# A graph attention layer on one core: softplus beside the layer norm, edge values on VectorE, scatters one slot earlier, the residual two steps later, q2/k2 evictions behind the score maxima

## The chip, the core and the metric

The kernel runs on one core of a Trainium2 chip. The core has five engines that each work through a queue of their own in program order: TensorE (PE, with its weight loads listed as PEld), VectorE (DVE), ScalarE (ACT), GpSimd (POOL) and SyncE (SP, which here only starts transfers). They meet at semaphores. The metric is the device time of one execution in microseconds. Before the change the median of 3 runs is 320.62 us (320.31 to 321.89).

## What is computed

The input x is 384 nodes by 1024 features. All of it is float32.

```python
h = max(layernorm(x), 0)
q, k, v = h @ wq.T + bq, h @ wk.T + bk, h @ wv.T + bv
q2, k2, v2 = (q @ wiq.T + biq), (k @ wik.T + bik), (v @ wiv.T + biv)     # 16 heads of 64
mask = full((384, 384), -inf)
mask[src, dst] = softplus(edge_weights)[edge_type - 1]                   # 6528 edges
mask[i, i]     = softplus(edge_weights)[3] where it is still -inf
scores = q2 @ k2.T / 8 + mask
out = x + (softmax(scores) @ v2) @ wo.T + bo
```

An edge may occur more than once; the kernel makes one occurrence count by looking for repeated keys, and sends the others to a dump cell.

## The kernel before

**Precision and matmuls.** Every weight block of 128 x 1024 (a "chunk") and every activation is split into a high and a low part (`split_hi` on ScalarE, line 77; `split_lo`, line 82, on VectorE or GpSimd), and each product is three matmuls (`mm3`, lines 358 to 360). There are 56 chunks in the order v, q (8 each), iv (8), k (8), eight pairs of iq and ik, o (8). A chunk is a "slot" w: 0 to 7 are v, 8 to 15 q, 16 to 23 iv, 24 to 31 k. Slot w begins with `slot_head(w)`: the high split of w+2, the eviction of slot w-1 (`evac_row`: VectorE writes f, line 373; ScalarE the high part, line 374; VectorE the low part, line 375, after the next low split), the low split of w+2, and the load of w+4. PSUM has three banks with the name g; in the iv phase one of them holds one of the six accumulators, so that in the k phase two are in turn.

**The mask** is made beside the projections. `mask_detect` (line 211, one VectorE instruction for each of the 51 columns of 128 edges) looks for repeated keys. After each nine, `mask_index` (lines 217 and 218) writes the target cells. Then one indirect transfer for each column, started by GpSimd (`mask_scatter`, line 222), puts the 128 values into one of three tables in HBM. Columns take turns over the tables, so that scatter i waits for the landing of scatter i-3. `detect(s)` lays this out by slot: softplus in slots 0 to 2, its values on GpSimd (lines 165 to 168), the diagonal (`mask_base`, lines 204 and 206) in slot 3, detections from slot 2, three scatters in each slot from slot 4. In iv step 5, behind the 51st scatter, `mask_load` (line 232) reads the tables back into `mbs`; `mask_select` (line 236) copies them into `ma` on VectorE at the end of slots 24 (two) and 25 (one).

**The residual.** x + bo is made in HBM in six pieces: `residual(k)` in iv step k starts a load, an addition on VectorE (line 496) and a store of three successive pieces, in two buffers.

**Attention.** 48 steps, three for each of 16 heads. Step i: scores S(i) on TensorE (line 665, two banks), then VectorE adds the mask and takes the maxima (`do_ttr(i-1)`, line 671), ScalarE exp (line 675), VectorE and GpSimd the norm (`do_norm(i-3)`, lines 679 and 680), TensorE transposes (`do_T(i-5)`, line 685, two banks), ScalarE and VectorE evict them (`do_pt(i-6)`, lines 694 and 695), TensorE multiplies with v2 once a head (`do_A`, line 702). Between them `fill(r)` puts in other matmuls, in units of three with the pace RATE for each step: the iq and ik chunks (`fill_qk`), then the output projection (`fill_o`), whose pieces are released at set steps (`wready`, XSTEP + 3 = 44). At the start of an iq or ik chunk `fill_qk` also puts out the splits of w+2 and the eviction of the chunk before (`qk_done`, lines 368 and 369, and four transfers), at that place in all queues. `wo_prep` splits the o chunks in steps 37, 38, 41, 44, 47 and 51.

All of it is written with a manual schedule: each engine's queue has the order of the program text.

Of the kernel before, what the change touches and what calls it, by code (L numbers as in the profile page):

```python
# [22 lines left out]
def gnn_kernel(ctx: ExitStack, tc: tile.TileContext, x, edges, erows, etw, wq, wk, wv, wiq, wik, wiv, wo,  # L23
# [13 lines left out]
    ctx.enter_context(tc.manual_schedule())  # L37

    EB = 8
    DS, GI = 2, 3  # L40
    NTAB, RNG = 3, EC // 3
    WARM = 20

# [46 lines left out]
    xall = G3.bitcast(F32).rearrange("p a k n -> p (a k n)")  # L90
    xt = [xall[:, t * D:(t + 1) * D] for t in range(NT)]
    xn = [xall[:, (NT + t) * D:(NT + t + 1) * D] for t in range(NT)]
    for t in range(NT):
        nc.sync.dma_start(xt[t], x[t * 128:(t + 1) * 128, :])
    load(0)
    ert = work.tile([128, N], F32, tag="e", name="er", bufs=EB)
    er = ert[:EC, :256].bitcast(I32).rearrange("p (a j) -> p a j", a=2)
    nc.scalar.dma_start(er, erows)
    ed = const.tile([128, 3 * EC], I32, name="ed")
    nc.sync.dma_start(ed, edges)  # L100
    load(1)
# [33 lines left out]
        nc.gpsimd.memset(zero, 0.0)  # L135

    def mask_fill():
        nc.gpsimd.memset(ma, -3.0e38)
        for j in range(NT):
            nc.gpsimd.tensor_scalar(ma[:, j, j * 128:(j + 1) * 128], ident, 3.0e38, -3.0e38, op0=OP.mult, op1=OP.add)  # L140

    def table_clear(g):

        nc.sync.dma_start(tabs[g][:CELLS, :].rearrange("(j p m) o -> p j (m o)", p=128, m=N),
                          zero[:, None, :].to_broadcast([128, NT, N]))

    def mask_keys():
        nc.gpsimd.tensor_copy(ed.bitcast(F32), ed)
        nc.gpsimd.tensor_scalar(tmpe[:, 0, :], tmpe[:, 0, :], float(N), None, op0=OP.mult)
        nc.gpsimd.tensor_tensor(key, tmpe[:, 0, :], tmpe[:, 1, :], OP.add)  # L150

    def softplus_a():
        nc.vector.tensor_scalar(w8[:, 0:4], ew, 0.0, None, op0=OP.max)
        nc.vector.scalar_tensor_tensor(w8[:, 4:8], ew, -1.0, ew, op0=OP.mult, op1=OP.min)
        nc.scalar.activation(w8[:, 4:8], w8[:, 4:8], AF.Exp)

    def softplus_b():
        nc.scalar.activation(w8[:, 4:8], w8[:, 4:8], AF.Ln, bias=1.0)

    def softplus_c():  # L160
        nc.scalar.activation(sq, epsc, AF.Exp)
        nc.vector.tensor_tensor(w8[:, 4:8], w8[:, 4:8], w8[:, 0:4], OP.add)
        nc.vector.tensor_scalar(w8[:, 4:8], w8[:, 4:8], 8.0, 1.0e-37, op0=OP.mult, op1=OP.max)
        t, ty = tmpe[:, 0, :], tmpe[:, 2, :]
        nc.gpsimd.tensor_scalar(val, ty, 0.0, w8[:, 7:8], op0=OP.is_equal, op1=OP.mult)
        for i in range(4):
            nc.gpsimd.tensor_scalar(t, ty, float(i + 1), w8[:, 4 + i:5 + i], op0=OP.is_equal, op1=OP.mult)
            nc.gpsimd.tensor_tensor(val, val, t, OP.add)

    krt = work.tile([128, N], F32, tag="e", name="kr", bufs=EB)  # L170
    kf = ert[:EC, :256].rearrange("p (a j) -> p a j", a=2)

    def key_rows_a():
        nc.gpsimd.tensor_copy(kf, er)
        nc.gpsimd.tensor_scalar(kf[:, 0, :], kf[:, 0, :], float(N), None, op0=OP.mult)

    def key_rows_b():
        nc.gpsimd.tensor_tensor(krt[:EC, :128], kf[:, 0, :], kf[:, 1, :], OP.add)
        nc.sync.dma_start(krow, krt[:EC, :128])

    rows = {}
    PA = 6
# [51 lines left out]
    def mask_select(g):  # L234

        nc.vector.copy_predicated(ma, mbt[g].bitcast(I32), mbt[g])
# [64 lines left out]
    def warm(n):  # L301
        for i in range(n):
            ps = bank("g")
            nc.tensor.transpose(ps[:, :128], ident, ident)

    warm(WARM)
    key_rows_a()
    key_rows_b()
    load(2)
    for s in range(NTAB):  # L310
        key_load(0, s)
# [44 lines left out]

    def mm3(ps, lhi, llo, rhi, rlo, first, last):
# [62 lines left out]

    def detect(s):

        if s == 0:
            softplus_a()
        if s == 1:
            softplus_b()
        if s == 2:
            softplus_c()
        if s == 3:
            mask_base()  # L430
        if s < NTAB:
# [11 lines left out]
        if s == DS + 12:  # L443
            biv_load()

    nde = [0]
# [68 lines left out]

    def v2_evac(i):
# [23 lines left out]
    def qk_done(w):  # L540
# [12 lines left out]
        else:  # L553
# [4 lines left out]
                    nc.sync.dma_start(kf[r * 64:(r + 1) * 64, o, :, :], nf[o * 64:(o + 1) * 64, :, :])  # L558
            stacks["k", p] = ks

    def fill_qk():
        nonlocal w
        lo_sel = 0
# [24 lines left out]

# [27 lines left out]

    OT = [(0, 0), (0, 1), (1, 0), (1, 1), (2, 0), (2, 1)]
    OREADY, XSTEP = 17, 41
    now = [0]
    wready = [0, 0] + [99] * 6  # L620

    def ysum(a, c=(0, 512)):
# [115 lines left out]
    for i in range(S + LA + 4):  # L738
# [87 lines left out]
```

## Time and profile before

| | before |
|---|---|
| median of 3 runs | 320.62 us |
| the profiled execution, its own time | 321.02 us |
| its span | 319.3 us |
| PE busy | 296.7 us (93%) |
| PEld, DVE, ACT, POOL busy | 279.9, 202.4, 153.8, 167.2 us |
| the 51 scatters on POOL (line 222) | 56.8 us, mean 1114 ns |
| TensorE clock granted | full, but for one of the 40 slices |

The span runs from the first to the last instruction of the profiled execution, and the execution's own time is 1.7 us more. A busy share of PE is an average: what counts is where PE's queue has holes, and which wait ends each of them last. In the lines of a timeline the columns are start and duration in microseconds, engine, line, operation, output<-input with shapes, the number of instructions, and in brackets the idle time before and what ended it.

### The profile page before, as it was taken

What the parts mean: (1) busy time and instruction counts of PE and PEld (TensorE: products, weight loads), DVE (VectorE), ACT (ScalarE), POOL (GpSimd) and SP (SyncE); (2) the same over time, 40 slices, a digit from 0 to 9 for tenths busy, and PEclk for the clock granted to TensorE, in tenths of its full rate; (3) what the DMA queues carried; (4) which work ended last, traced back from release to release, by engine and by line L of the source; (5) the groups of instructions that cost most, each with busy time, mean ns of one, the idle gap of its engine ahead of it and who ended that gap; (6) DMA issues with size and microseconds to landing.
All of it is one profiled execution on the core that took longest, in us unless ns stands there. A gap on an engine that the chain in (4) does not pass through costs nothing.

```text
span 319.3 us, 4955 instructions
## 1 busy us (share of the span) xinstructions
PE 296.7 (93%) x1643; PEld 279.9 (88%) x1643; DVE 202.4 (63%) x487; ACT 153.8 (48%) x286; POOL 167.2 (52%) x170
## 2 busy tenths in 40 slices
PE   5999999999999993499999898999989999999995
PEld 4899999999888892499999888999889999888884
DVE  2886999987633230899932447675666685896413
ACT  2647254333322120255453466777677776876300
POOL 3692876767664756033333334563736578657010
PEclk9999999999999999599999999999999999999999
DMA  7899566445964683533348946464646475940005
GB/s 256 255 273 372 195 216 219 148 127 190 293 194 141 185 308 88 194 133 135 104 141 224 267 143 166 116 164 117 167 118 162 117 182 166 274 156 0 2 0 197
DMA packets 22197, 55.12 MB, mean 173 GB/s; under 512 B 4534, under 2 KB 8220, under 8 KB 22172
## 3 DMA queue, kind: packets, MB, share of 16 engines
q1 hardware_dynamic: 20054, 52.96, 53.9%
q0 software_dynamic: 2064, 1.80, 2.0%
q8 instruction: 13, 0.21, 0.3%
q14 instruction: 12, 0.10, 0.1%
q10 hardware_dynamic: 54, 0.05, 0.1%
HBM read 40.39 MB, written 4.97 MB: 142 GB/s over the span
## 4 chain that ended last, share of the span: by engine, by line
PE 66%; DMA 16%; POOL 5%; issue 5%; DVE 4%; ACT 2%; SPq 0%; POOLq 0%; DVEq 0%
PE g L358 16%; PE g L360 16%; PE g L359 16%; DMA tab<-val,idx 12%; PE a L702 5%; PE s L665 5%; PE t L685 5%; POOL tab L222 4%; DMA mbs<-tab 2%; DMA g<-in_x_dram 1%; DVE whl L82 1%; PE g L404 1%; DMA qs<-nat 1%; ACT nat L368 1%; DVE lnt L246 1%
## 5 line engine op out<-in xcount | busy, mean ns | idle before, releaser
L358 PE MATMUL g<-g,whl 128*128 128x384 f32 x312 | 107.6, 345 | 9.9 <-DVE f L373 9.9
L360 PE MATMUL g<-g,whl 128*128 128x384 f32 x312 | 105.3, 337 | 0.0
L359 PE MATMUL g<-g,whl 128*128 128x384 f32 x312 | 105.0, 337 | 0.0
L222 POOL DMA_INDIRECT tab<-val,idx x51 | 56.8, 1114 | 28.3 <-DMA tab<-val,idx 13.5
L358 PEld LDWEIGHTS g<-g,whl 128*128 128x128 f32 x312 | 59.3, 190 | 10.2 <-issue 10.2
L77 ACT ACTIVATE whl<-raw 128x1024 fp32r<-128x1024 f32 x51 | 53.4, 1050 | 26.2 <-DMA raw<-in_wk_dram 13.7
L680 POOL TENSOR_TENSOR e<-e,s 128x384 f32<-128x384 f32 x48 | 39.3, 828 | 49.8 <-DVE s L679 43.9
L359 PEld LDWEIGHTS g<-g,whl 128*128 128x128 f32 x312 | 59.4, 190 | 0.0
L360 PEld LDWEIGHTS g<-g,whl 128*128 128x128 f32 x312 | 59.1, 190 | 0.0
L82 DVE TENSOR_TENSOR whl<-raw,whl 128x1024 fp32r<-128x1024 f32 x41 | 50.0, 1219 | 9.1 <-ACT whl L77 9.1
L374 ACT ACTIVATE g<-f,bc 128x384 fp32r<-128x384 f32 x24 | 14.8, 617 | 63.0 <-DVE f L373 63.0
L675 ACT ACTIVATE e<-e,s 128x384 f32<-128x384 f32 x48 | 29.4, 612 | 13.5 <-DVE s L671 13.3
L82 POOL TENSOR_TENSOR whl<-raw,whl 128x1024 fp32r<-128x1024 f32 x11 | 27.1, 2463 | 15.1 <-ACT whl L77 13.6
L695 DVE TENSOR_TENSOR pt<-t,pt 128x384 fp32r<-128x384 f32 x48 | 26.3, 548 | 7.6 <-ACT pt L694 6.7
L369 DVE SCALAR_TENSOR_TENSOR nat<-g,bc,nat 128x384 fp32r<-128x384 f32 x16 | 9.9, 617 | 33.3 <-ACT nat L368 33.3
L665 PE MATMUL s<-ks,qs 128*128 128x384 f32 x96 | 25.2, 344 | 5.0 <-DVE s L671 5.0
L694 ACT ACTIVATE pt<-t 128x384 fp32r<-128x384 f32 x48 | 23.1, 481 | 9.7 <-PE t L685 9.4
L671 DVE CUSTOM_DVE_ANT_0 e<-s,ma 128x384 f32<-128x384 f32 x48 | 26.2, 548 | 1.1 <-PE s L665 0.9
L665 PEld LDWEIGHTS s<-ks,qs 128*128 128x128 f32 x96 | 17.2, 188 | 7.4 <-DVE s L671 6.6
L685 PE MATMUL t<-ident,e 128*128 128x128 f32 x144 | 23.5, 271 | 0.0
L375 DVE SCALAR_TENSOR_TENSOR g<-f,bc,g 128x384 fp32r<-128x384 f32 x24 | 21.1, 884 | 0.7 <-ACT g L374 0.7
L524 POOL TENSOR_TENSOR vhl<-tv,vhl 128x512 fp32r<-128x512 f32 x6 | 9.2, 1537 | 23.3 <-ACT vhl L523 23.3
(147 smaller groups left out, 435.7 us busy)
## 6 DMA issues: line engine op xcount, KB each, us to landing
ks<-nat SPq DMA_DIRECT2D x32, 192.0 KB, 3.5
raw<-in_wv_dram SPq DMA_DIRECT2D x8, 512.0 KB, 6.3
raw<-in_wq_dram SPq DMA_DIRECT2D x8, 512.0 KB, 3.5
raw<-in_wiv_dram SPq DMA_DIRECT2D x8, 512.0 KB, 4.1
raw<-in_wk_dram SPq DMA_DIRECT2D x8, 512.0 KB, 5.2
raw<-in_wiq_dram SPq DMA_DIRECT2D x8, 512.0 KB, 3.4
raw<-in_wik_dram SPq DMA_DIRECT2D x8, 512.0 KB, 4.0
raw<-in_wo_dram SPq DMA_DIRECT2D x8, 512.0 KB, 4.7
```

What stands on the lines that cost most here:

```text
L77: nc.scalar.activation(dst[0], raw[w], AF.Copy)
L82: (eng or nc.vector).tensor_tensor(lo, raw[w], hi.bitcast(F32), OP.subtract)
L222: nc.gpsimd.indirect_dma_start(out=tabs[c // RNG], out_offset=bass.IndirectOffsetOnAxis(ap=idx[:, c:c + 1], axis=0), in_=val[:, c:c + 1], ...
L358: nc.tensor.matmul(ps, lhi, rhi, start=first, stop=False)
L359: nc.tensor.matmul(ps, lhi, rlo, start=False, stop=False)
L360: nc.tensor.matmul(ps, llo, rhi, start=False, stop=last)
L665: nc.tensor.matmul(ps[:, :N], qs[:, o, t * 128:(t + 1) * 128], ks[:, o, s, :], start=(s == 0), stop=(s == 1))
L671: nc.vector.tensor_tensor_reduce(e, st_ps.pop(i)[:, :N], ma[:, t, :], -0.125, 3.0e38, OP.add, OP.min, s[:, 0:1])
L675: nc.scalar.activation(es[i], es[i], AF.Exp, bias=s[:, 0:1], scale=-1.0, accum_out=s[:, 1:2])
L680: nc.gpsimd.tensor_tensor(es[i], es[i], s[:, 2:3].to_broadcast([128, N]), OP.mult)
L685: nc.tensor.transpose(ps[:, k * 128:(k + 1) * 128], es[i][:, k * 128:(k + 1) * 128], ident)
L695: nc.vector.tensor_tensor(lo, pv, hi.bitcast(F32), OP.subtract)
```

## The change

The parts, in the order of the program:

- The edge rows are loaded as 128 x 102 instead of 51 x 256 values, by SP behind the first tile of x instead of by ScalarE; `key_rows` works on that form and writes the same keys to HBM. `mask_consts` moves to the start of GpSimd's queue.
- Softplus: `softplus_a` goes between the low parts of the layer norm on VectorE; Exp, Ln and the Exp that restores the table follow each other on ScalarE behind the high split of chunk 1; `softplus_c` follows on VectorE.
- The values of the edges (nine instructions on 128 x 51) go from GpSimd to VectorE, in slot 1. The low splits of chunks 3 and 4 go from VectorE to GpSimd.
- Detections are 3 in slot 1, 6 in slot 2, then 4; scatters start in slot 3; `mask_load` stands in iv step 4.
- `mask_fill` and `mask_base` go from GpSimd's queue ahead of the scatters to right behind `mask_load`.
- `residual(k)` runs in slot 18 + k, the last two in k slots 0 and 1.
- In the attention the head of an iq or ik chunk becomes a task, run in each step behind `do_norm`. RATE goes from 7.6 to 7.9.

```diff
+    ert = work.tile([128, N], F32, tag="e", name="er", bufs=EB)
+    er = ert[:, :2 * EC].bitcast(I32)
     for t in range(NT):
         nc.sync.dma_start(xt[t], x[t * 128:(t + 1) * 128, :])
+        if t == 0:
+            nc.sync.dma_start(er, erows)
     load(0)
-    ert = work.tile([128, N], F32, tag="e", name="er", bufs=EB)
-    er = ert[:EC, :256].bitcast(I32).rearrange("p (a j) -> p a j", a=2)
-    nc.scalar.dma_start(er, erows)
...
+    def mask_floats():
+        nc.gpsimd.tensor_copy(ed.bitcast(F32), ed)
+
     def mask_keys():
-        nc.gpsimd.tensor_copy(ed.bitcast(F32), ed)
...
-        nc.scalar.activation(w8[:, 4:8], w8[:, 4:8], AF.Exp)
-
     def softplus_b():
+        nc.scalar.activation(w8[:, 4:8], w8[:, 4:8], AF.Exp)
         nc.scalar.activation(w8[:, 4:8], w8[:, 4:8], AF.Ln, bias=1.0)
+        nc.scalar.activation(sq, epsc, AF.Exp)
...
+    def mask_values():
         t, ty = tmpe[:, 0, :], tmpe[:, 2, :]
-        nc.gpsimd.tensor_scalar(val, ty, 0.0, w8[:, 7:8], op0=OP.is_equal, op1=OP.mult)
+        nc.vector.tensor_scalar(val, ty, 0.0, w8[:, 7:8], op0=OP.is_equal, op1=OP.mult)
         for i in range(4):
-            nc.gpsimd.tensor_scalar(t, ty, float(i + 1), w8[:, 4 + i:5 + i], op0=OP.is_equal, op1=OP.mult)
-            nc.gpsimd.tensor_tensor(val, val, t, OP.add)
+            nc.vector.tensor_scalar(t, ty, float(i + 1), w8[:, 4 + i:5 + i], op0=OP.is_equal, op1=OP.mult)
+            nc.vector.tensor_tensor(val, val, t, OP.add)
...
+    mask_consts()
     warm(WARM)
-    key_rows_a()
-    key_rows_b()
+    key_rows()
...
     ln_lo(2, 0, p2[0])
+    softplus_a()
     ln_lo(0, 1, p0[1])
     ln_lo(1, 1, p1[1])
     ln_lo(2, 1, p2[1])
     ln_rstd()
+    mask_floats()
     split(1, nc.gpsimd)
-    mask_consts()
+    softplus_b()
+    softplus_c()
     mask_keys()
-    mask_fill()
...
-        split_lo(w + 2)
+        split_lo(w + 2, nc.gpsimd if w in (1, 2) else None)
...
     def detect(s):
-        if s == 0:
-            softplus_a()
         if s == 1:
-            softplus_b()
-        if s == 2:
-            softplus_c()
-        if s == 3:
-            mask_base()
+            mask_values()
...
-        if s == DS:
-            detects(5)
-        elif s > DS:
-            detects(4)
-        if s >= DS + 2:
+        detects((0, 3, 6)[s] if s < 3 else 4)
+        if s >= 3:
             scatters(3)
...
         scatters(3)
-        residual(k)
-        if k == 5:
+        if k == 4:
             mask_load()
+            mask_fill()
+            mask_base()
+        if k >= 2:
+            residual(k - 2)
...
         for g in {0: (0, 1), 1: (2,)}.get(m, ()):
             mask_select(g)
+        if m < 2:
+            residual(m + 6)
...
+    tasks = []
+    def run_tasks():
+        while tasks:
+            tasks.pop(0)()
+    def qk_head(w):
+        load(w + 4)
+        split_hi(w + 2)
+        if pendq:
+            pendq.pop(0)()
+        split_lo(w + 2, nc.gpsimd if (w + 2) % 2 == PAR else None)
     def fill_qk():
         nonlocal w
         for p in range(8):
             for n in ("iq", "ik"):
-                load(w + 4)
-                split_hi(w + 2)
-                if pendq:
-                    pendq.pop(0)()
-                split_lo(w + 2, nc.gpsimd if (w + 2) % 2 == PAR else None)
+                tasks.append(lambda w=w: qk_head(w))
+                if now[0] < 0:
+                    run_tasks()
...
-        pendq.pop(0)()
+        tasks.append(lambda: pendq.pop(0)())
...
-    PRE, RATE, RATE_O, RATE_E = 84, 7.6, 8, 8
+    PRE, RATE, RATE_O, RATE_E = 84, 7.9, 8, 8
...
             do_norm(i - 3)
+        run_tasks()
         if 0 <= i - LT < S:
             do_T(i - LT)
```

More of the change, by code (lines that the diff above doesn't have):

```diff
@@ L39, in gnn_kernel @@
     EB = 8
-    DS, GI = 2, 3
+    GI = 3
     NTAB, RNG = 3, EC // 3
@@ L154, in softplus_a, with softplus_b, key_rows @@
         nc.vector.scalar_tensor_tensor(w8[:, 4:8], ew, -1.0, ew, op0=OP.mult, op1=OP.min)
+    def softplus_b():
         nc.scalar.activation(w8[:, 4:8], w8[:, 4:8], AF.Exp)
-    def softplus_b():
         nc.scalar.activation(w8[:, 4:8], w8[:, 4:8], AF.Ln, bias=1.0)
+        nc.scalar.activation(sq, epsc, AF.Exp)
     def softplus_c():
-        nc.scalar.activation(sq, epsc, AF.Exp)
         nc.vector.tensor_tensor(w8[:, 4:8], w8[:, 4:8], w8[:, 0:4], OP.add)
         nc.vector.tensor_scalar(w8[:, 4:8], w8[:, 4:8], 8.0, 1.0e-37, op0=OP.mult, op1=OP.max)
+    def mask_values():
         t, ty = tmpe[:, 0, :], tmpe[:, 2, :]
-        nc.gpsimd.tensor_scalar(val, ty, 0.0, w8[:, 7:8], op0=OP.is_equal, op1=OP.mult)
+        nc.vector.tensor_scalar(val, ty, 0.0, w8[:, 7:8], op0=OP.is_equal, op1=OP.mult)
         for i in range(4):
-            nc.gpsimd.tensor_scalar(t, ty, float(i + 1), w8[:, 4 + i:5 + i], op0=OP.is_equal, op1=OP.mult)
-            nc.gpsimd.tensor_tensor(val, val, t, OP.add)
+            nc.vector.tensor_scalar(t, ty, float(i + 1), w8[:, 4 + i:5 + i], op0=OP.is_equal, op1=OP.mult)
+            nc.vector.tensor_tensor(val, val, t, OP.add)
     krt = work.tile([128, N], F32, tag="e", name="kr", bufs=EB)
-    kf = ert[:EC, :256].rearrange("p (a j) -> p a j", a=2)
-    def key_rows_a():
+    kf = ert[:, :2 * EC]
+    def key_rows():
         nc.gpsimd.tensor_copy(kf, er)
[L175 to L179, printed above, removed]
+        nc.gpsimd.tensor_scalar(kf[:, :EC], kf[:, :EC], float(N), None, op0=OP.mult)
+        nc.gpsimd.tensor_tensor(krt[:, :EC], kf[:, :EC], kf[:, EC:], OP.add)
+        nc.sync.dma_start(krow.rearrange("c j -> (c j)").rearrange("(p e) -> p e", p=128), krt[:, :EC])
     rows = {}
@@ L436, in detect @@
             key_load(2, s - 7)
-        if s == DS:
-            detects(5)
-        elif s > DS:
-            detects(4)
-        if s >= DS + 2:
+        detects((0, 3, 6)[s] if s < 3 else 4)
+        if s >= 3:
             scatters(3)
-        if s == DS + 12:
+        if s == 14:
             biv_load()
@@ L559, in qk_done @@
             stacks["k", p] = ks
+    tasks = []
[8 more added lines that the diff above has]
+        split_lo(w + 2, nc.gpsimd if (w + 2) % 2 == PAR else None)
     def fill_qk():
         nonlocal w
-        lo_sel = 0
         for p in range(8):
             for n in ("iq", "ik"):
-                load(w + 4)
-                split_hi(w + 2)
-                if pendq:
-                    pendq.pop(0)()
-                split_lo(w + 2, nc.gpsimd if (w + 2) % 2 == PAR else None)
+                tasks.append(lambda w=w: qk_head(w))
+                if now[0] < 0:
+                    run_tasks()
                 gps[w] = bank("g")
@@ L618, in gnn_kernel @@
     OREADY, XSTEP = 17, 41
-    now = [0]
+    now = [-1]
     wready = [0, 0] + [99] * 6
@@ L805 @@
             [np.asarray(a).reshape(EC, 128).T for a in (src, dst, edge_type_5)], axis=1)),
-        "erows": np.ascontiguousarray(np.stack([np.asarray(a).reshape(EC, 128) for a in (src, dst)], axis=1)),
+        "erows": np.ascontiguousarray(np.concatenate([np.asarray(a).reshape(128, EC) for a in (src, dst)], axis=1)),
         "etw": np.asarray(L0_gnn_edge_type_weights),
```

## The prediction, made before the changed kernel ran

> **What bounds the kernel now.** PE is busy for 93% of the span, so I read first who PE waits for: the waits of its queue, longest in total first (total, times, longest, in us).
>
> ```profile
> PE g L358 <- DVE f L373: 9.9, 1, 9.9
> PE s L665 <- DVE s L671: 5.0, 5, 1.6
> ```
>
> Beyond the first 14 us only these two reasons make holes. The first is one hole. PE's timeline shows it:
>
> ```profile
> 122.02 0.34 PE L360 MATMUL g<-g,whl 128*128 128x384 f32 x1
> 132.23 0.66 PE L358 MATMUL g<-g,whl 128*128 128x384 f32 x1 [9.87 <-DVE f L373]
> ```
>
> The columns are start, duration, engine and line, operation, and the idle time before. The matmul at 132.23 would have started at 122.20 (pitch 0.173 us elsewhere): 10.0 us lost. The 14 matmuls after it take 4.3 us, not 2.4: another 1.9. The hole costs 11.9. VectorE's timeline says why: its queue stood before the mask.
>
> ```profile
> 128.28 1.43 DVE L236 COPY_PREDICATED ma<-mbs 128x1152 f32<-128x1152 int32 x1 [12.27 <-DMA mbs<-tab]
> 130.21 1.43 DVE L236 COPY_PREDICATED ma<-mbs 128x1152 f32<-128x1152 int32 x1 [0.51 <-DMA mbs<-tab]
> 131.54 0.54 DVE L373 TENSOR_TENSOR f<-g,rrow 128x384 f32<-128x384 f32 x1
> ```
>
> The f at 131.54 frees the bank that slot 26 needs. Before it stand the table reads, and before those the scatters. GpSimd's timeline, the scatters 1, 28, 37, 46 and 51 and the reads:
>
> ```profile
> 39.09 1.26 POOL L222 DMA_INDIRECT tab<-val,idx  x1 [0.36 <-DVE junk L211]
> ...
> 80.04 0.96 POOL L222 DMA_INDIRECT tab<-val,idx  x1 [0.31 <-issue]
> ...
> 97.28 0.96 POOL L222 DMA_INDIRECT tab<-val,idx  x1 [2.00 <-DMA tab<-val,idx]
> ...
> 111.52 0.96 POOL L222 DMA_INDIRECT tab<-val,idx  x1 [0.30 <-issue]
> ...
> 122.92 0.96 POOL L222 DMA_INDIRECT tab<-val,idx  x1 [0.30 <-issue]
> 123.88 2.37 POOL L232 DMA_DIRECT2D mbs<-tab  x3
> ```
>
> So 1.52 us for each of the first 27, 1.75 over the next 18, 2.28 over the last five. The floor is 0.96 + 0.30 of issue; the rest is mostly landings (2.1 to 6.2 us), for which the third scatter after waits. The five holes in the attention have this form on VectorE:
>
> ```profile
> 177.11 0.62 DVE L369 SCALAR_TENSOR_TENSOR nat<-g,bc,nat 128x384 fp32r<-128x384 f32 x1 [3.89 <-ACT nat L368]
> 177.64 1.22 DVE L82 TENSOR_TENSOR whl<-raw,whl 128x1024 fp32r<-128x1024 f32 x1
> 178.77 0.55 DVE L671 CUSTOM_DVE_ANT_0 e<-s,ma 128x384 f32<-128x384 f32 x1
> ```
>
> The eviction waits for a chunk's end with a split behind it, and the maxima that free the bank stand behind both. By PE's start times the five cost 5.8 us.
>
> **What the Trainium skill says.** "TensorE: Matmul & The Clock Gate", Part 1: after an idle window of about 3.4 us PE's clock is halved, for about as long. The trace agrees (0.32 for 0.173 us after 9.87 idle; nothing after holes up to 1.6). "SBUF — State Buffer", Who interferes with whom: VectorE and GpSimd share a port pair under an exclusive lock, taken by tensor_scalar, or by two SBUF inputs against a reading GpSimd instruction. The trace agrees: a tensor_scalar on 128x3 (line 259) takes 2.02 us beside a GpSimd low split. "ScalarE: Activation LUTs", What ACT_TABLE_LOAD costs: 1.28 us plus a drain; here 1.28, and 1.5 with the small activation. "DMA: Bandwidth & Descriptors", Issuing engines are not separate DMA queues: all transfers share 16 engines, which fits the landings.
>
> **The change part by part.**
>
> *Start.* The erows issue ahead of x tiles 1 and 2 delays them by some 0.45 us; VectorE took x0 and x1 without a pause, so up to 0.5 reaches PE. `mask_consts` fits into 4.1 us of GpSimd's idle time. I take +0.2 (0 to 0.5).
>
> *Softplus.* ScalarE: three table loads with their activations, 3 x 1.5 = 4.5 us, from 15.8 to 20.2; then the high split of chunk 2 to 21.2, its low split to 22.4. Slot 2 needs it at 23.1. Cost nothing, with 0.6 us of cover.
>
> *Values and first detections.* VectorE from f(0) at 22.7: f 0.55, nine value instructions some 1.5 (0.15 to 0.2 each, from lines 162 and 163), nine detections 2.65, f 0.55, two low parts 1.1, index 0.45: 29.5. To that comes the lock: GpSimd's low splits of chunks 3 and 4 (2.4 each, from 22.4 and about 25) block the tensor_scalars by 1.6 to 4 us. The index is ready at 31 to 33.5; f(1) comes by 30.2 (slot 4 needs it at 31.3), the low split of chunk 5 by 35.2 (needed at 35.5): hidden, narrowly. GpSimd is free at 27.4, so the first scatter goes out at about 32.5 instead of 39.1.
>
> *Scatters.* 27 x 1.52 bring the 28th to 73.5. The next nine now come before the residual traffic (from about 85): 9 x 1.52, 87.1. The last 14 run beside it as 18 did before: 14 x 1.75 = 24.5. The 51st starts at 111.6. At 1.52 throughout it would be 108.4; with 2.28 at the end and a late start, 115.5.
>
> *Fill and diagonal.* Off the queue's start they hid; now they follow the reads. From the 51st: 0.96 + 2.37 (reads) + 2.4 (line 138, 140) + 2.7 (lines 204, 206: three pairs of 0.9) = 8.4. The reads land sooner (5.4 and 7.2 before). Two selects 2.8, a residual addition 0.6, f 0.55: 12.4 from the 51st to the free bank, 9.2 before. So f ends at 124.0, and PE, out of work at 122.4, idles 1.7 us, too short for the clock. Gain 11.9 - 1.9 = 10.0. A 51st at 108.4 gives the whole 11.9; at 115.5 PE idles 5.5, perhaps half the clock loss: gain 5.5.
>
> *Residual.* Each piece takes some 5.7 us (its load waits for the store two pieces earlier, about 5 us to land). SP can start at 85.2 instead of 79.3, so the last addition can run at 118, before the second select ends at 122.8: hidden. The low splits behind the additions had 4 us and more of cover (6 for chunk 26). In v2_evac the second tv waits for the last store, landing at about 128: up to 1 us of VectorE, within its slack.
>
> *Evictions behind the maxima.* The maxima no longer stand behind them, so the five holes go: -5.8. What is late next are the transposes' low parts behind eviction and split: end of chunk + 0.6 + 0.62 + 1.22 + 0.55 = 3.0 us, when the next transpose can ask for the bank 2.1 us later: 0.8, expected once or so.
>
> *RATE 7.9.* PE gets 384 - 84 = 300 units in 38.0 steps, not 39.5. But the output pieces are held until step 44: steps 41 to 43 are left without filler. At the last eviction, now in step 37, it also stands before VectorE's cast of o chunk 2. From S(37): chunk end 1.0, eviction 2.3, low part 2.9, aof 3.4, cast 4.1; then GpSimd as here:
>
> ```profile
> 265.82 2.40 POOL L82 TENSOR_TENSOR whl<-raw,whl 128x1024 fp32r<-128x1024 f32 x1 [1.38 <-issue]
> 268.17 0.83 POOL L680 TENSOR_TENSOR e<-e,s 128x384 f32<-128x384 f32 x1
> 268.95 1.01 POOL L718 TENSOR_TENSOR g<-aof,g 128x384 fp32r<-128x384 f32 x1
> 269.92 2.41 POOL L82 TENSOR_TENSOR whl<-raw,whl 128x1024 fp32r<-128x1024 f32 x1
> ```
>
> and norm(36) 0.83: 11.6. PE reaches T(36) after 9.4 (10.2 before, when the norm was there after 9.0). So PE waits 2.2 us. I take +2.2 (0 to 3), and +0.5 for small waits. Attention: -5.8 + 0.8 + 2.7 = -2.3 (-5 to 0).
>
> Sum: +0.2 - 10.0 - 2.3 = -12.1. Against the profiled execution: span 319.3 to 307.2, its time 321.02 to 308.9. The median lies 0.4 lower: 320.62 - 12.1 = 308.5 us.
>
> **Rivals.**
>
> *Landings set the pace.* The scatters start earlier into the table clears and key rows, and the last 14 meet the residual's stores; at 2.28 us each they end at 119 and f at 131.4: the hole is 9 us with its clock loss, gain about 1 there and 2.3 in the attention: 317. For it: 2.28 at the end before. Against: 1.58 from 37 to 46, beside the same residual. Halfway, a 51st at 115.5: 313.
>
> *All hidden.* 51st by 109 and no wait in step 41: -11.9 - 5 + 0.2, about 304. For it: nine undisturbed scatters ran at 1.41 (67.3 to 80.0). Against: 12.4 us from scatter to bank, and no filler in three steps.
>
> *Slower: the mask's tail on GpSimd.* Fill and diagonal add 3.2 us between last scatter and bank. If the scatters end as late as before because landings alone set them, f ends at 135.3, 3.2 later; without a gain in the attention that is 324. It decides from a 51st at about 123, with 2.3 gained elsewhere from 124. Against: a start 6 us earlier must all be lost.
>
> **How the numbers follow.** Likeliest case 0.62 (own range 305.5 to 312); landings 0.22 (312 to 318); all hidden 0.10 (303 to 305.5); slower 0.06. Together 304.5 to 315 holds eight in ten, leaving out the ends of the second and third and the last. Within 0.5% (1.6 us, about what a measurement tells from no change) falls little of the landings case: 0.03; slower 0.05; faster 0.92.
>
> **What would show it.** First scatter at 31 to 34, 51st at 108 to 115.5; the hole before slot 26 under 4 us with full clock after; selects released by GpSimd's line 212 and not by the reads; no wait of PE for the maxima; a wait of about 2 us for a norm near step 41. A 51st after 119, or new holes in slots 2 to 7, would make the forecast wrong.

## The result, and the profile after

The changed kernel takes 318.98 us (median of 22 runs, 316.21 to 321.44); the kernel before, on the same chips, 320.5 us (22 runs, 318.0 to 323.79). The ratio is 0.9953, with the interval 0.993 to 0.9977: 1.5 us faster, where 12.1 had been forecast. The medians here and in the table below are over all runs; the ratios leave out the runs that took over 1.5% more than the fastest of their kernel. The profiled execution has a span of 317.1 us (319.3 before) and took 318.8 us.

PE's queue first, as before: what it waits for (total, times, longest, in us).

```profile
PE g L366 <- DVE f L381: 8.2, 1, 8.2
...
PE t L699 <- POOL e L694: 2.6, 2, 1.7
...
PE t L699 <- DVE pt L709: 0.8, 1, 0.8
```

The wait for the maxima is gone altogether. The transposes now wait for the norms (line 694) and once for an eviction. And the wait for f, which was to fall under 2 us, is still there: PE's timeline shows the same hole in the same place.

```profile
122.72 0.34 PE L368 MATMUL g<-g,whl 128*128 128x384 f32 x1
131.23 0.66 PE L366 MATMUL g<-g,whl 128*128 128x384 f32 x1 [8.17 <-DVE f L381]
```

By start times 8.3 us are lost, and 2.0 in slow matmuls behind it: 10.3. Before it was 12.1, not the 11.9 of the forecast: the 4.3 us behind that hole hold 13 matmuls, which take 2.25 at full speed, and not 14. The mask's own chain on GpSimd (the scatters 1, 28, 37 and 51, the first and third table read, the fill, the end of the diagonal):

```profile
34.06 1.24 POOL L228 DMA_INDIRECT tab<-val,idx  x1 [6.37 <-DVE idx L224]
...
76.65 0.96 POOL L228 DMA_INDIRECT tab<-val,idx  x1 [2.00 <-DVE g L383]
...
91.55 1.91 POOL L228 DMA_INDIRECT tab<-val,idx  x1 [2.17 <-DMA tab<-val,idx]
...
116.41 0.96 POOL L228 DMA_INDIRECT tab<-val,idx  x1 [0.30 <-issue]
117.37 0.83 POOL L238 DMA_DIRECT2D mbs<-tab  x1
...
121.71 0.75 POOL L238 DMA_DIRECT2D mbs<-tab  x1 [2.54 <-DMA tab<-val,idx]
122.44 1.08 POOL L140 MEMSET ma<- 128x1152 f32 x1
...
126.66 0.45 POOL L212 TENSOR_TENSOR ma<-ma,d 128x128 f32<-128x128 f32 x1
```

And what VectorE does with it:

```profile
127.14 2.90 DVE L242 COPY_PREDICATED ma<-mbs 128x1152 f32<-128x1152 int32 x2 [13.45 <-POOL ma L212]
129.94 0.68 DVE L495 TENSOR_TENSOR xh<-xh,bot 128x512 f32<-128x512 f32 x1
130.53 0.55 DVE L381 TENSOR_TENSOR f<-g,rrow 128x384 f32<-128x384 f32 x1
```

The 51st scatter starts 6.5 us earlier than before (116.41 for 122.92), but f ends only 1.0 earlier (131.08 for 132.08). From the 51st to the end of f it was 9.2 us and is 14.7; I call this stretch the tail. The new link is at 121.71: the third table read waits for the 51st scatter to land, 5.3 us behind its start, and fill and diagonal stand in GpSimd's queue behind that read. In the kernel before, the three reads went out in one piece without a wait, so the last landing took 2.6 us at most (122.92 to the third read at 125.49). The DMA engines tell the two stretches apart. From the 51st scatter to the third read, before and then after (stretch, length, busy time of PE, PEld, DVE, ACT and POOL with instructions, PE clock, DMA share, GB/s):

```profile
122.92:125.49 2.57, 0.00 (x0) 0.00 (x0) 0.00 (x0) 0.00 (x0) 2.56 (x4) 1.00 0.14 13
```

```profile
116.41:121.71 5.30, 5.30 (x33) 5.30 (x32) 0.00 (x0) 0.00 (x0) 2.56 (x4) 1.00 0.83 260
```

Three differences make up the span's: hole with its slow matmuls -1.8, attention -1.1 (five holes of 5.8 gone, 4.7 come), start +0.7 (the matmul behind the hole was due at 122.89, not 122.20). Together -2.2, and the span fell by 2.2.

### The profile page after: what moved, and what is told of

Its sections match the earlier page's. It is cut to its first block, busy times and chain, and to the rows that moved or that the text cites. A ratio compares the mean times of both kernels' runs of the same rounds, so it can differ in the third digit from the quotient of the medians.

```text
span 317.1 us, 4954 instructions
## 1 busy us (share of the span) xinstructions
PE 297.0 (94%) x1643; PEld 279.4 (88%) x1643; DVE 204.3 (64%) x494; ACT 154.8 (49%) x286; POOL 166.5 (53%) x163
## 4 chain that ended last, share of the span: by engine, by line
PE 69%; DMA 12%; issue 6%; POOL 6%; DVE 3%; ACT 3%; SPq 0%; DVEq 0%; POOLq 0%
PE g L366 17%; PE g L368 17%; PE g L367 17%; DMA tab<-val,idx 10%; PE a L716 5%; PE s L679 4%; PE t L699 4%; POOL tab L228 3%; DMA g<-in_x_dram 2%; PE g L412 2%; POOL e L694 1%; ACT nat L376 1%; DVE whl L82 1%; DVE pt L709 1%; ACT e L689 1%
## 5 line engine op out<-in xcount | busy, mean ns | idle before, releaser
L228 POOL DMA_INDIRECT tab<-val,idx x51 | 58.2, 1141 | 31.5 <-DMA tab<-val,idx 12.1
L694 POOL TENSOR_TENSOR e<-e,s 128x384 f32<-128x384 f32 x48 | 40.2, 846 | 49.0 <-DVE s L693 43.1
L82 DVE TENSOR_TENSOR whl<-raw,whl 128x1024 fp32r<-128x1024 f32 x39 | 47.6, 1221 | 13.5 <-ACT whl L77 13.5
L82 POOL TENSOR_TENSOR whl<-raw,whl 128x1024 fp32r<-128x1024 f32 x13 | 32.0, 2460 | 17.5 <-ACT whl L77 13.0
L699 PEld LDWEIGHTS t<-ident,e 128*128 128x128 f32 x144 | 18.2, 140 | 7.7 <-POOL e L694 3.2
L376 ACT ACTIVATE nat<-g,bc 128x384 fp32r<-128x384 f32 x16 | 9.3, 582 | 26.2 <-PE g L368 20.2
```

The source lines that it names most:

```text
L82: (eng or nc.vector).tensor_tensor(lo, raw[w], hi.bitcast(F32), OP.subtract)
L228: nc.gpsimd.indirect_dma_start(out=tabs[c // RNG], out_offset=bass.IndirectOffsetOnAxis(ap=idx[:, c:c + 1], axis=0), in_=val[:, c:c + 1], ...
L694: nc.gpsimd.tensor_tensor(es[i], es[i], s[:, 2:3].to_broadcast([128, N]), OP.mult)
L699: nc.tensor.transpose(ps[:, k * 128:(k + 1) * 128], es[i][:, k * 128:(k + 1) * 128], ident)
```

## The experiments

The table gives, for every kernel, the scatters and f in its profiled execution, and the sum of the waits for landings that GpSimd's timeline shows ahead of the last 14 scatters (each with the 0.3 us of issue that every scatter has). All in us; "tail" is the 51st start to the end of f.

| kernel | 1st | 28th | 37th | 51st | waits, last 14 | tail | PE hole | median | ratio to before (interval) |
|---|---|---|---|---|---|---|---|---|---|
| before | 39.1 | 81.3 | 98.6 | 122.9 | 6.2 | 9.2 | 10.0 | 320.5 | |
| changed | 34.1 | 76.7 | 91.6 | 116.4 | 5.2 | 14.7 | 8.3 | 318.98 | 0.9953 (0.993 to 0.9977) |
| e1 fill early | 34.9 | 78.5 | 94.6 | 119.1 | 5.5 | 12.1 | 8.6 | 317.48 | 0.987 (0.9791 to 0.9949) |
| e2 RATE 7.6 | 33.6 | 77.3 | 92.7 | 116.3 | 3.5 | 13.8 | 8.4 | 316.23 | 0.9873 (0.9795 to 0.9951) |
| e3 no residual | 33.8 | 76.8 | 92.0 | 112.7 | 2.4 | 13.2 | 3.2 | 311.1 | 0.9672 (0.9596 to 0.9748) |
| e4 six tables | 33.6 | 70.8 | 89.5 | 107.5 | 0.0 | | | 336.92 | 1.0496 (1.0433 to 1.0559) |
| e5 no additions | 33.0 | 76.6 | 93.0 | 119.4 | 9.0 | 11.4 | 10.0 | 319.55 | 0.9975 (0.9949 to 1.0) |
| e6 residual back | 34.3 | 76.4 | 92.0 | 119.0 | 8.8 | 11.8 | 8.5 | 319.86 | 0.9982 (0.9954 to 1.0009) |
| e7 residual late | 33.9 | 77.3 | 90.8 | 110.9 | 1.4 | 13.3 | 2.2 | 314.44 | 0.9813 (0.9737 to 0.9888) |
| e8 four together | 34.0 | 76.2 | 90.5 | 110.4 | 0.8 | 13.7 | 2.3 | 309.3 | 0.9672 (0.9622 to 0.9723) |
| e10 the same, residual a step earlier | 33.6 | 77.3 | 92.4 | 112.7 | 4.0 | 11.2 | 2.5 | 307.78 | 0.9594 (0.956 to 0.9628) |
| e11 the same, fill behind the reads | 32.8 | 75.2 | 89.1 | 109.3 | 1.5 | 13.3 | 1.7 | 306.66 | 0.9573 (0.953 to 0.9615) |
| f1 before + attention part | 38.5 | 78.7 | 96.3 | 121.1 | 7.8 | 9.4 | 8.2 | 319.98 | 0.999 (0.9964 to 1.0016) |
| f1b before + attention part, RATE 7.6 | 38.9 | 79.8 | 97.1 | 121.9 | 6.3 | 8.9 | 9.0 | 316.03 | 0.9841 (0.9786 to 0.9895) |
| f2 before + residual late | 39.0 | 79.9 | 94.2 | 114.7 | 3.7 | 10.2 | 2.9 | 316.29 | 0.9866 (0.9824 to 0.9908) |
| f3 = f1b + f2 | 39.0 | 82.5 | 97.0 | 119.1 | 5.2 | 8.9 | 6.1 | 312.45 | 0.9719 (0.9667 to 0.9771) |

The profiled executions of e1, e3, e4 and f3 took clearly longer than their medians (320.13, 314.38, 341.38 and 316.57 us), so their rows may show a later 51st than most of their executions have. All but the last two columns are of one execution.

### Is it the fill and the diagonal behind the reads? (e1)

```diff
+        if s == 2:
+            mask_fill()
+            mask_base()
...
             mask_load()
-            mask_fill()
-            mask_base()
```

> The changed kernel, with the fill and the diagonal of the mask put into GpSimd's queue before the first scatter (in its idle time from 27.7 to 34.1) and not behind the three table reads. Theory: behind the 51st scatter's landing (121.4) two things stand in a row, the third table read and then the fill and diagonal, and the selects wait for the second. With them early the selects are released by the table read, f ends about 9.3 behind the start of the 51st scatter in place of 14.7, TensorE's hole at the mask falls from 8.3 to 3-4 and its slow matmuls with it: 4 to 6.5 us faster than the changed kernel, 312.5 to 315. Rival, landings alone: the last read lands where the fill and diagonal end anyhow, and the time moves by 1 us at most, 318 to 319.

317.48 us: 1.5 us under the changed kernel's median, with intervals that overlap, and so neither of the two. The trace shows why the question stayed open. GpSimd's timeline and then VectorE's:

```profile
122.63 2.42 POOL L238 DMA_DIRECT2D mbs<-tab  x3 [2.60 <-DMA tab<-val,idx]
```

```profile
127.03 1.43 DVE L242 COPY_PREDICATED ma<-mbs 128x1152 f32<-128x1152 int32 x1 [13.32 <-DMA mbs<-tab]
```

The tail did fall from 14.7 to 12.1, and the selects are released by the reads, as expected. But even the first read waited until 122.63, and in this execution the 51st stood at 119.1, 2.7 later; the hole stayed at 8.6. The place at the front may have a cost of its own: the first scatter waits for VectorE's index in both traces, and it starts at 34.9 with the fill beside VectorE's values and at 34.1 without.

### Is it the residual? (e3, e5, e6)

e3 leaves the residual's bias out of the computation (the last stage adds x alone), e5 leaves out the additions of bo only, e6 has the residual at the steps of the kernel before.

```diff
# e3
-        if k >= 2:
-            residual(k - 2)
...
-        if m < 2:
-            residual(m + 6)
...
-            nc.sync.dma_start(xb[t], xbd[t * 128:(t + 1) * 128, :])
+            nc.sync.dma_start(xb[t], x[t * 128:(t + 1) * 128, :])
# e5
-                nc.vector.tensor_tensor(xh[i], xh[i], xh["b"][:, c], OP.add)
# e6
-        if k >= 2:
-            residual(k - 2)
+        residual(k)
...
-        if m < 2:
-            residual(m + 6)
```

> The changed kernel without the addition of the bias bo to x and without its stores (this part of the computation is left out; the last stage adds x alone). Theory: the last 14 scatters run at 1.77 us because VectorE's residual adds and their stores share SBUF and the queues with GpSimd's descriptor work; without them 1.5 each, the 51st at about 112.5 in place of 116.4, and 3.5 to 5 us off the time. Rival: the pace of the scatters is their own (landings, or GpSimd's work on the descriptors); the 51st moves by less than 1 us and the time by less than 1.

> The changed kernel without VectorE's six additions of bo in the residual (left out of the computation); its loads of x, of bo and its stores stay. Leaving out the whole residual put the 51st scatter at 112.7 in place of 116.4. Theory: the scatters' landings queue behind the residual's 256 KB loads and stores; without the adds alone the 51st stays at 115.5 to 117.5 and the time within 1.5 us of the changed kernel. Rival: the adds on VectorE hold GpSimd up (six adds of 0.68 us, one beside every second or third scatter); the 51st comes to 112 to 114 and the time falls by 4 to 9.

> The changed kernel with the residual's loads, adds and stores two steps earlier, where the kernel before has them. Theory: the traffic delays the landings wherever it meets them, so the 51st scatter stays at 115 to 117; but the last stores are gone when the last scatter lands and the table reads run, so f ends 12.5 behind the 51st in place of 14.7: hole 5.5 to 6.5, 2 to 4 us faster than the changed kernel. Rival: the place makes no difference (within 1 us).

Without the residual the 51st starts at 112.7, as the theory had it, and the time falls by 7.9 us, more than expected. Up to the 37th scatter nothing differs (92.0 for 91.6). The last 14 take 20.8 us for 24.9: of the 4.1 us saved, 2.0 are idle time of GpSimd between the scatters (5.9 for 7.9), and 2.1 are the scatters' own instructions (14.9 for 17.0). e5 tells the additions from the transfers. Without the additions the scatters' instructions are short too (14.5), but the idle time grows to 11.8, and the time stays (319.55): shorter instructions buy nothing while landings are late. The last scatter of all waited longest. GpSimd's timeline of e5:

```profile
119.35 0.96 POOL L228 DMA_INDIRECT tab<-val,idx  x1 [3.34 <-DMA raw<-in_wk_dram]
```

So it is not VectorE's additions, which the theory of e3 had named as well; it is the transfers. The wait is put down to a weight load, which is the last transfer to end, not one that a scatter depends on; 119.35 is outside the 115.5 to 117.5 that I had expected, on the side of the theory.

e6 misses the theory's 2 to 4 us: at its old place the residual costs the same (319.86, waits of 8.8 us in the last 14). Its last stores are gone earlier, and the tail is shorter (11.8), but the last 14 scatters take 27.1 us for 24.9; the two steps that the change moves the residual by are worth nothing that shows.

SyncE's timeline of the changed kernel shows what the 51st scatter (116.41) has to land among:

```profile
114.77 0.33 SPq L493 DMA_DIRECT2D xh<-in_x_dram  x1
115.15 1.63 SPq L65 DMA_DIRECT2D raw<-in_wk_dram  x1
116.87 0.38 SPq L497 DMA_DIRECT2D xbd<-xh  x1
117.34 0.38 SPq L65 DMA_DIRECT2D raw<-in_wk_dram  x1
```

That is 256 + 512 + 256 + 512 KB issued within 2.6 us. From 117 to 123 the engines moved 303 GB/s; at this rate the 1.57 MB are worth 5.2 us, by estimate, and the landing took 5.3. A third of it, 512 KB, is the residual's.

### The residual behind the mask (e7), also alone on the kernel before (f2)

```diff
-        if k >= 2:
-            residual(k - 2)
...
-        if m < 2:
-            residual(m + 6)
+        residual(m)
...
-                t = work.tile([128, 2, N], F32R, tag="nat", name="xh", bufs=2)
-                xh[i] = t.bitcast(F32).rearrange("p a n -> p (a n)")[:, :512]
+                xh[i] = xh["r"][i % 2]        # the spare 2 KB of the two bias tiles
```

> The changed kernel with the whole residual six steps later, in the eight steps of the k projection, behind the mask (its three transient tiles lie in the spare 2 KB of the two bias tiles). Theory: as without the residual, the last scatters run free of its traffic, the 51st at 112 to 113.5, hole at the mask 0 to 3.5: 308.5 to 312. Rival: VectorE's adds and the loads then delay the k projection, which gives 2 us or more back: 312 to 316, with new waits of TensorE between 135 and 165.

> The kernel before, its scatters starting at 39.1 as ever, with the residual alone moved behind the mask into the steps of the k projection. Theory: the 28th scatter stays at 81.3 and the 23 behind it take 34 us in place of 41.6, so the 51st stands at 115 to 116.5 in place of 122.9; behind it 12 to 13.5 us of landing, reads and selects, because the weight loads now go on: f at 128 to 129.5, hole at the mask 6 to 7.5 in place of 10, 3 to 5.5 us faster than before. Rival: the early start of the scatters is what is needed; without it the late residual gives less than 2 us.

All of the computation is there again, and the 51st starts at 110.9. The work by stretches of the changed kernel, and then of e7, from 92 to 110 us (stretch, length, busy time of PE, PEld, DVE, ACT and POOL with instructions, PE clock, DMA share, GB/s):

```profile
92.00:110.00 18.00, 18.00 (x81) 14.90 (x80) 8.13 (x9) 4.24 (x4) 12.78 (x11) 1.00 0.62 184
```

```profile
92.00:110.00 18.00, 18.00 (x81) 14.90 (x80) 4.90 (x4) 4.26 (x5) 12.96 (x14) 1.00 0.40 124
```

TensorE does the same; the DMA engines are busy 0.40 of the time in place of 0.62, and GpSimd gets 14 instructions off in place of 11. The hole is 2.2 us, and the matmuls behind it run at full clock. The median is 4.5 us under the changed kernel's, not the 7 to 10 expected: it lies in the rival's range. TensorE has two new waits, 0.6 us at 150 for VectorE's f and 1.7 at 166 for the first shifted copies of k2, which is the 2 us that the rival named.

f2 puts the same move alone on the kernel before, with the scatters starting at 39.0 as before. 316.29 us, 4.1 faster, within the 3 to 5.5 expected: the 51st at 114.7 is earlier than in the changed kernel, which starts 5 us sooner. Over all profiled executions the waits of the last 14 scatters are 3.5 to 9.0 us with the residual beside them and 0.8 to 4.0 without, but for f3 with 5.2. The hole (2.9) is smaller than expected, because the tail was 10.2 and not 12 to 13.5.

### The attention (e2, f1, f1b)

```diff
-    PRE, RATE, RATE_O, RATE_E = 84, 7.9, 8, 8
+    PRE, RATE, RATE_O, RATE_E = 84, 7.6, 8, 8
```

e2 is this line on the changed kernel. f1 is the kernel before with the tasks and 7.9, f1b with the tasks and 7.6.

> The changed kernel with RATE 7.6 in place of 7.9 (the spacing by which the planner of the attention steps spreads its tasks). Theory: the 3.1 us that TensorE waits for the norms of two late steps (270 and 273), and the 1.6 for eviction and maxima, come from the plan running ahead of GpSimd's norms; by the rows of the trace 1.4 to 2 us of the 4.7 stay. 2.5 to 3 us faster than the changed kernel, 316. Rival: the norms are late because GpSimd is slow, whatever the plan; the time stays within 0.5 us.

> The kernel before with the attention part of the change alone (evictions of q2/k2 as tasks behind the maxima, RATE 7.9). The prediction gave this part 2.3 us; the rows of the changed kernel give 5.8 less 4.7 = 1.1. Theory: 1 us faster than before (319.5, ratio 0.997), the five waits for the maxima gone and the two for the norms (1.7 and 0.9) there as in the changed kernel. Rival: the norms are late only behind the changed front of the kernel; without it 2 to 4 us faster.

> The same with RATE 7.6, the value of the kernel before. Theory: 5.8 less 1.6 = 4.2 us faster than before (316.4, ratio 0.987): the reordering is worth what it removes, and the step from 7.6 to 7.9 gives most of it away. Rival: RATE is worth less than 1 us here, ratio 0.994 or more.

PE's waits in f1:

```profile
PE t L695 <- POOL e L690: 2.6, 2, 1.7
...
PE t L695 <- DVE pt L705: 0.8, 1, 0.8
```

and in f1b:

```profile
PE t L695 <- DVE pt L705: 1.2, 2, 0.8
```

The same two waits for norms as in the changed kernel, behind another front; so they belong to this part. By start times the waits of the attention are 4.7 us in f1 and 1.5 in f1b. With 7.9 the part is worth nothing that can be told from no change (0.999); with 7.6 4.4 us by the medians (0.9841). e2 took 3.1 us off the attention's waits in its trace (4.7 to 1.6), and its median stands 2.7 under the changed kernel's, though with overlapping intervals. The theory holds in all three: the reordering is good, and the step of RATE that came with it pays most of it back.

### The landings' own pace (e4)

Every second group of three scatters goes to three spare tables, which nothing reads, so half of the edges are missing from the mask.

```diff
+    spare = [dram.tile([CELLS + 128, 1], F32, name=f"spare{g}") for g in range(NTAB)]
...
-        nc.gpsimd.indirect_dma_start(out=tabs[c // RNG],
+        nc.gpsimd.indirect_dma_start(out=(spare if i // NTAB % 2 else tabs)[c // RNG],
```

> The changed kernel with every second group of three scatters sent to three spare tables, which are neither cleared nor read (so half of the edges are left out of the mask); a scatter then waits only for the landing of the sixth before it, not of the third. Theory 'landings set the pace': 1.3 to 1.4 us each in place of 1.58 to 1.77, the 51st at 98 to 105, TensorE's hole at the mask is gone, and 8 to 10.5 us come off. Theory 'GpSimd's own work sets the pace': 1.5 to 1.75 each as before, the 51st at 113 to 117 and less than 3 us off.

As to the scatters the first theory is right: 1.38 us each up to the 28th (1.58 in the changed kernel) without one wait for a landing, and the 51st at 107.5, although the 37th stood 6.6 us waiting for VectorE. As to the time both are wrong: 336.92, 18 us more than the changed kernel. PE's waits:

```profile
PE g L367 <- issue: 7.3, 11, 1.8
...
PE g L369 <- issue: 6.0, 7, 1.6
PE g L368 <- issue: 4.9, 7, 0.9
```

and ScalarE's timeline:

```profile
73.29 0.61 ACT L383 ACTIVATE g<-f,bc 128x384 fp32r<-128x384 f32 x1 [13.37 <-issue]
```

18.2 us in pieces of about one, and 13.4 in one, in which TensorE and ScalarE waited for nothing that the profile shows, between 53 and 111 us, while the DMA engines were 0.17 busy from 52 to 88. By start times TensorE loses some 28 us there, for its clock is down too (0.65 from 52 to 88); the mask's 10.3 are gone, and so about 18 remain. These stops come with six scatters in flight, and with three they are not there. By what way, these runs don't show; it stays open. What e4 does show is that with three in flight landings set the scatters' pace and not GpSimd's work, and that the spare tables are no way out.

### Together (e8, e10, e11, f3)

e8 is e7 with the early fill of e1, RATE 7.6 and the edge rows' load back on ScalarE's queue; e10 has the residual one step earlier on top; e11 is e10 with fill and diagonal behind the reads again, where the change has them. f3 is f1b and f2 in one, without anything the change does ahead of the mask.

```diff
# e8, ahead of load(0)
-        if t == 0:
-            nc.sync.dma_start(er, erows)
+    nc.scalar.dma_start(er, erows)
# e10
+        if k == 7:
+            residual(0)
...
-        residual(m)
+        if m < 7:
+            residual(m + 1)
# e11
-        if s == 2:
-            mask_fill()
-            mask_base()
...
             mask_load()
+            mask_fill()
+            mask_base()
```

> Late residual, fill and diagonal before the first scatter, RATE 7.6, and the load of the edge rows back on ScalarE's queue. Theory: hole at the mask gone and TensorE's clock full (10 off), attention waits 1.4 to 2 in place of 4.7 (2.6 to 3 off), start 0.5 to 0.7 earlier: 304 to 307. If the landings of the last scatters still set the end of the mask, 307 to 311.

> As with all four together (309.3), with the residual one step earlier: its first loads in the last step of the iv projection, its last store one step before the end of the k projection. Theory: the 1.4 us that TensorE waits for the first shifted copies of k2 at 167 are due to the last residual store and its buffers; they go, 307.5 to 308.5. Rival: that wait is that of the copies themselves, 309 to 310; or the first loads meet the table reads and the hole at the mask grows by up to 1 us.

> The fastest version so far (late residual one step earlier, RATE 7.6, edge rows on ScalarE's queue), with fill and diagonal behind the table reads again, where the change has them. Theory: fill and diagonal end 5.3 behind the last read's issue, the first two reads land about 4.5 behind it when the weight loads go on; so the selects come 1 to 5 us later than with the early fill, f ends at 125 to 128 in place of 123.9, 1 to 4 us slower (309 to 312). Rival: landings alone set it, within 0.7 us.

> The kernel before with the late residual and the attention part at RATE 7.6, without everything the change does ahead of the mask (scatters from 39.1 as before). The two alone gave 4.3 and 5.1. Theory: they add, since one is the mask's hole and one the attention's waits: 310.5 to 312, so that the earlier scatters are worth 3 to 4 us of the fastest version's 307.8. Rival: the gains overlap, 313 or more.

e8 gave 309.3 us, which is the second of its two expectations, that landings still set the end of the mask: a hole of 2.3 us was left. In e10 the wait for the copies at 166 us fell from 1.4 to 0.3, as expected, and the time to 307.78. e11 answers the question of e1 for the time: with fill and diagonal behind the reads it is not slower (306.66; the intervals of e10 and e11 overlap, and the ratios are 0.7 us apart). The theory is out, the rival right as to the time. GpSimd's timeline of e11:

```profile
109.28 0.96 POOL L227 DMA_INDIRECT tab<-val,idx  x1 [1.49 <-DMA bot<-in_x_dram]
...
112.97 0.75 POOL L237 DMA_DIRECT2D mbs<-tab  x1 [1.12 <-DMA tab<-val,idx]
```

and VectorE's:

```profile
118.44 3.13 DVE L241 COPY_PREDICATED ma<-mbs 128x1152 f32<-128x1152 int32 x2 [6.20 <-POOL ma L211]
122.05 0.56 DVE L380 TENSOR_TENSOR f<-g,rrow 128x384 f32<-128x384 f32 x1
```

The selects are released by the diagonal at 118.4, 5.5 us behind the last read's issue. In e10, with the fill early, they start at 118.2, only 1.5 behind it. So the fill does lengthen the tail (13.3 for 11.2), but in e11's trace the 51st stands 3.5 us earlier, at 109.3. Of these 0.8 are there from the first scatter on (32.8 for 33.6), as between e1 and the changed kernel; where the rest comes from, one trace of each doesn't show. In e8, with the fill early too, the selects waited for the reads until 120.5, 5.3 behind the last one.

f3 has a median of 312.45, a little above the expected 310.5 to 312; by its ratio, 0.9719, it is 311.5, inside. The gains add up: by their ratios f2 and f1b save 4.3 and 5.1 us, and f3 saves 9.0. So all that the change does ahead of the mask (softplus, values, the scatters 5 us earlier) is worth 4.0 to 4.7 us by the ratios (f3 against e10 and e11, which have the edge rows on ScalarE's queue and the k2 copies earlier as well), once the residual is out of the way and RATE is put back. The interval of f3 alone is 1.7 us to either side.

e11 beats both kernels: 306.66 us, 4.3% under the kernel before.

## Why the prediction was wrong

**The step that failed is the mask's end: "The 51st starts at 111.6" and "12.4 from the 51st to the free bank".** It gave f at 124.0; f ended at 131.1, late by 4.8 at the 51st and by 2.3 behind it. The hole gave back 1.8 us where 10.0 were forecast: 8.2 of the 9.9 us that are missing between the profiled executions.

- *Start of the scatters*, 32.5 forecast: 34.06, +1.6. The lock is a part of it. The Trainium skill ("SBUF — State Buffer", Who interferes with whom) has VectorE and GpSimd share a port pair that a tensor_scalar can take for itself. The trace agrees: the two of them beside GpSimd's low splits took 1.73 and 2.39 us (0.24 otherwise), 3.6 lost, near the upper end of the 1.6 to 4 that I gave and 0.8 above its middle. The other 0.8 I have not traced.
- *"27 x 1.52"*: a miscount of mine. The rows called the 28th, 37th and 46th are the 27th, 36th and 45th of the kernel before. 40.95 us for 26 steps are 1.575 each, and the changed kernel has 1.577. +1.6. With the right count the chain says 113.7, so this slip alone doesn't explain the miss. It is in two other figures: the last stretch before has six steps, so 1.90 us each and not 2.28, and the undisturbed scatters from 67.3 to 80.0 have eight, so 1.59 and not 1.41.
- *"9 x 1.52"*: 1.66. +1.2. *"14 x 1.75"*: 1.78. +0.4. These four make the 51st 4.8 late.
- *The tail*: the terms of fill, diagonal, selects, addition and f were right within 0.4 us in sum. Missing was a wait: the third read for the 51st's landing, 2.5 us and a pause of 0.2 before. I had written that "the reads land sooner", and had asked this of the reads only, not of the landing which they wait for.

**What the sum held at nothing: "Residual ... hidden".** I priced its additions on VectorE and the arrival of its pieces. Its transfers share the DMA engines with the landings that the scatters and reads wait for. e3 and e7 show what that costs: 3.7 and 5.5 us at the 51st scatter, f at 125.9 and 124.2 in place of 131.1, and 7.9 and 4.5 us of the time. The kernel before has the same loss, and f2 gets 4.1 us back from it without any earlier scatter. A part of this was in the forecast without my seeing it: "14 x 1.75" was measured beside the residual, and it came nearly right. So the residual is no further term of the 4.8 us; it is a cost that the forecast carried along, and it bears on the tail's missing wait. That f in e7 falls on the forecast's 124.0 is luck: there the last 14 scatters took 20.1 us in place of 24.5, which makes up for a 37th that is 3.7 late and a tail that is 0.9 longer.

**The short tail before was no property of the mask.** I took 9.2 us from the kernel before and added the fill. But its 51st came at 122.9, when the transfers were nearly over: the last two weight loads went out at 113.5 and 116.0, and SP starts the next at 133.2. In the changed kernel the last of them went out at 117.3, behind the 51st, and the next at 132.2. It is not TensorE that ends the loads (it ran until 122.4 and 123.1); in both kernels VectorE has stood still before the selects, since 116.0 and 113.7. Split at the third read, the tails of the fifteen kernels with three scatters in flight fall into groups:

- From the 51st to the third read it is 2.6 to 3.0 us where the DMA engines are 0.09 to 0.26 busy (before, f1, f1b, f3, e5, e6), and 3.7 to 5.3 where they are 0.58 to 0.96 busy (all others, e1 among them). That the traffic does it is argued from these shares; no run took the weight loads away.
- From the third read to the first select it is 5.4 to 5.5 us wherever fill and diagonal stand behind the reads, and 0.8 to 3.3 where they come early, but for e8 with 5.3, where the reads themselves were late.

**Fill and diagonal.** 3.2 us on the tail by the forecast; e1 showed 2.6 and the pair of e10 and e11 2.2, between e7 and e8 it was nothing (13.3 and 13.7). In the time no pair shows a cost that is clear of the intervals. The place matters less than the working said.

**The attention** was right in kind: five holes gone (5.8 us), a late low part (0.9 and three of 0.2, forecast 0.8 and 0.5), the wait for the norm near step 41 (2.0, forecast 2.2). A second wait for the next norm, 1.1 us, was not in the sum; so -1.1 in the trace in place of -2.3.

**The start** came 0.7 later in place of 0.2. In seven executions with the changed start the last matmul ahead of the hole begins between 120.7 and 122.7, in five with the start of before between 121.8 and 122.3, so 0.5 can't be read from one trace. In the three kernels with the edge rows on ScalarE's queue it is 120.9 to 121.7.

**Softplus** was hidden, as forecast: its three table loads, 1.28 us each, left no hole.

**The rivals.** "Landings set the pace" named the right mechanism, with 0.22. It put f at 131.4, and f came at 131.1, but by luck: its 51st, at 119 from the wrong 2.28, was 2.6 too late, and its tail of 12.4 was 2.3 too short. The time, 317 by that rival, was 318.98, since attention and start gave less. Of the signs named, the release of the selects by line 212, the absent wait for maxima and the wait for a norm came as written; the first scatter was at the edge, the 51st and the hole outside.

## What to carry to other kernels

A transfer that is hidden as to its own result is not free when something else waits for small landings on the same engines: ask for each transfer which wait on the critical chain it shares the DMA engines with, and move it to where no such wait is. A latency that was read where the large transfers were over (a DMA share of 0.14 here) is the latency of a quiet chip; when the change moves the wait to where they still run (0.83), price it from a stretch like that. And when a change reorders and retunes at once (here the tasks and RATE), cost the two apart. Count the steps of a stretch from the rows before dividing by them.

## What was not expected of the hardware

- With six indirect scatters in flight in place of three, TensorE stood for 18.2 us and ScalarE once for 13.4 us without a reason in the profile (e4).
- A landing of a 128-value scatter took 5.3 us beside 1.57 MB of other transfers (changed kernel), and 2.6 at most when the loads had stopped (before).
- The slow clock behind a hole comes sooner than I had it: idle times of 2.13, 2.37 and 2.77 us at the mask (e8, e10, f2) were followed by ten slow matmuls, 1.5 us in all, and 1.50 and 2.01 us (e11, e7) by none. The ten are not the first behind the hole: six, three and eight at full speed go ahead of them. The Trainium skill ("TensorE: Matmul & The Clock Gate", Part 1) speaks of an idle window of about 3.4 us; here 2.1 was enough. Holes of 8 to 10 us were followed by 10 to 18 slow matmuls (1.7 to 2.8 us), and one of 3.0 (e3) by 18, so that their length says little.
